# A four-layer graph network on one core: layer 2 with transposed scores and a constant shift, and direct row sums for the last graph

## The chip, the cores and the metric

The kernel runs on one core of a Trainium2 chip. A core has TensorE (matrix products, PE in the profile, with its weight loads as PEld), VectorE (DVE), ScalarE (ACT), GpSimd (POOL) and SyncE (SP, which only issues transfers here), and 16 DMA engines. The engines run their own queues in order and wait for one another by semaphores. The metric is the device time of one launch in microseconds: before the change 3004.08 us, the median of three runs (3002.78 to 3010.93).

## The reference

There are 32 graphs of 512 nodes with 256 features. All share one 512x512 adjacency matrix, about 6% full and with a full diagonal. Four attention layers follow one another, each wrapped as x = layernorm(x + layer(x)). Layer 0 is an 8-head transformer block with a masked softmax and a small MLP. Layers 1 and 3 score an edge by a sum of two node terms under a leaky ReLU (one head in layer 1, four in layer 3). Layer 2, which the change rewrites, multiplies the features:

```python
h1 = inp @ W1; h2 = inp @ W2; h3 = inp @ W3
e = einsum('bnd,bmd->bnm', h1, h2)
e = leaky_relu(e, 0.2)
e = where(adj > 0, e, -1e12)
attention = softmax(e, axis=-1)
return relu(attention @ h3)
```

A softmax does not change when one constant is subtracted from all scores of a row; which constant is used matters only for the range of the exponentials.

## The kernel before

**Staging.** The weights, the adjacency (as edge_t, the transposed 0/1 matrix in bf16, and mask, a large number where there is no edge) and a few constants are prepared once by `prepare`. Then the function `graph` describes one graph: load x, run `layer0` to `layer3`, each followed by `normalise`, store. A graph's 512 nodes lie in four chunks of 128 partitions (NC = 4), its 256 features in two (KC = 2). All intermediates stay on chip, in numbered buffers of a few kinds: "p" (8 buffers of 128x2048, for the attention weights), "t", "y", "v", "e", "rs" and others, and eight PSUM banks of 128x512.

**Order of the work.** Nothing is issued while a layer is described. Each call of `plan` appends an operation with an engine, an assumed duration in ns, what it reads and writes, and, for transfers, an assumed time to landing (`lag`). `Plan.place` then simulates the engines and buffers and picks at each step the operation that can start first, with ties and urgency decided by a due time: the graph's number times PACE plus the due time of this operation within a graph, which a lone placement of one graph stretched by the table TENTHS gives. Up to five graphs (WAYS) are open at a time. START delays the first graphs' first operations, LAST shifts the due times of the last graphs, STAY is a penalty for a change of TensorE's tiling mode (operations carry a `tiling` number). So each engine's instruction order is fixed when the kernel is built; on the chip an engine only waits for semaphores.

**Layer 2** (line 1166): xT is transposed by TensorE (line 866), qT is its product with the combined matrix l2m = -W1 W2^T (line 879), v its product with W3 (line 893). For each chunk c of query nodes, line 1180 makes the negated scores with queries on the partitions; ScalarE makes 0.2 times them (line 1183), VectorE takes the minimum (line 1186), then adds the mask and finds each row's minimum in one instruction (line 1188), which is the row's maximum of the true scores. ScalarE takes the exponential with that as its bias and adds up each row (line 1193), and VectorE inverts the sum (line 1196). The second product needs the keys on the partitions, so 16 TensorE transposes a graph (line 1203) and four ScalarE evacuations (line 854) turn p into pT; line 1214 multiplies pT by v, and line 1219 applies the ReLU and the inverted sum.

**Layer 1** already builds its weights with keys on the partitions and gets row sums from a column of ones beside v (lines 1141, 1155, 1160).

**Row sums in layers 0 and 3.** Their exponentials also have keys on the partitions. The partial tiles p of a head group are added by accumulating DMAs from GpSimd (`add_dma`, line 934), in two levels; then a product with a one-hot matrix `pick` sums over the partitions (lines 1042 and 1269), followed by an evacuation, transposes (line 947) and a reciprocal.

**Range check.** The kernel keeps running minima of 0/1 tests in `fit`, `far` and `odd`; at the end they become one flag (line 1325 on), and if it is set, the slower `general_path` computes everything again.

Of the kernel before, what the change touches and what calls it, by code (L numbers as in the profile page):

```python
# [9 lines left out]
FP = mybir.dt.float32  # L10
# [7 lines left out]
P = 128  # L18
# [4 lines left out]
R_MIN, R_MAX = 1e-30, 1e20  # L23
H0, H3 = 8, 4
# [3 lines left out]
PACE = 90.76  # L28
START = (0, 0, 60.35, 91.65, 156.14)
LAST = ()  # L30
STAY = 3.96
TENTHS = (0, 30.43, 93, 94.94, 170.51, 206.64, 280.32, 312.71, 390.11, 381.83, 480.02)
# [411 lines left out]
class Plan:  # L444
# [62 lines left out]
    def place(self, urgency, ways, stay=0.0, run=True):  # L507


        held_by = {g: self.profile(g) for g in {self.ops[0].graph, self.ops[-1].graph}}  # L510
# [12 lines left out]
        def safe(op, kind, new):  # L523
            spare = len(free[kind]) - len(new)
            if spare < 0:
                return False
            have = spare
            for g in order:
                mine = held.get((g, kind), [])
                have += len(mine)  # L530
                if g == op.graph:
                    have += len(new)
                    mine = mine + new
                r, rows = front[g], held_by.get(g, held_by[self.ops[-1].graph])[kind]
                ahead = sorted(s.first for s in mine if s.first > r)
                for i, stop in enumerate(ahead + [len(rows)]):
                    if stop > r and max(rows[r:stop]) + len(ahead) - i > have:
                        return False
                    r = max(r, stop)
                if g == op.graph:  # L540
                    return True
# [70 lines left out]
def fast_path(  # L612
# [63 lines left out]
    nc.gpsimd.memset(eps, EPS)  # L676
    ones = const.tile([P, P], FP, name="ones")
# [47 lines left out]
    odd = keep("odd", [P, NC])  # L725

    def prepare():
        def load(dst, to, src, lag=3000):
            def run():
                with nc.allow_non_contiguous_dma(reason="columns, once"):  # L730
                    nc.sync.dma_start(to(T(dst[0] if isinstance(dst, tuple) else dst)), src)
            plan(SP, 450, run, [], [dst], lag=lag)
# [29 lines left out]
        for m in range(NC):  # L762
            bank = Slot("bank")

            def run(bank=bank, m=m):
                for c in range(NC):
                    nc.tensor.transpose(T(bank)[:, c * P:(c + 1) * P],
                                        T(edges)[:, c, m * P:(m + 1) * P], ident)
            plan(PE, 440, run, [edges], [bank])
            dve(690, lambda bank=bank, m=m: nc.vector.tensor_copy(T(edge_t)[:, m, :], T(bank)),  # L770
                [bank], [(edge_t, m)])

# [20 lines left out]
        for c in range(NC):  # L793
            off = Slot("e")
            dve(690, lambda c=c: nc.vector.tensor_scalar(
                T(mask)[:, c, :], T(raws[c // 2])[:, c % 2, :].bitcast(I32), 0.0, BIG, ALU.is_le, ALU.mult),
                [(raws[c // 2], c)], [(mask, c)])
            dve(690, lambda c=c, off=off: nc.vector.tensor_tensor(
                T(off), T(edges)[:, c, :], T(raws[c // 2])[:, c % 2, :].bitcast(I32), ALU.not_equal),
                [edges, (raws[c // 2], c)], [off])  # L800
            dve(690, lambda c=c, off=off: nc.vector.tensor_reduce(
                T(odd)[:, c:c + 1], T(off), mybir.AxisListType.X, ALU.max), [off], [(odd, c)])
# [34 lines left out]
        for k in range(KC):  # L837
            bank = Slot("bank")

            def run(bank=bank, k=k):  # L840
# [6 lines left out]
                T(l2m)[:, k, :], T(bank)[:, :C], AF.Copy, scale=-1.0), [bank], [(l2m, k)])  # L847
        load(l2w3, lambda t: t, rows(l2_w3))
        scored(l3w, l3_w, l3_a, H3)
# [154 lines left out]
    def layer0(xs):  # L1004
# [7 lines left out]
        oT, sm, totals = Slot("t"), Slot("bank"), []  # L1012
        for g in range(KC):
            av, ps = Slot("bank"), []
            for m in range(NC):
# [14 lines left out]
                if m % 2:  # L1030
                    add_dma(ps[m - 1], p)
                if m == 3:
                    add_dma(ps[0], ps[2])
                total = ps[0]

            totals.append(total)
            evac(oT, lambda t, g=g: t[:, g, :], av, lambda b: b, N, [(oT, g)])

        def run():
            for g, p in enumerate(totals):  # L1040
                for j in range(J):
                    nc.tensor.matmul(T(sm)[j * 32:(j + 1) * 32, :], pick[:, g, :], T(p)[:, j, :],  # L1042
                                     start=(g == 0), stop=(g == KC - 1))
        plan(PE, 1740, run, totals, [sm], tiling=2)
# [3 lines left out]
        def check():  # L1048
            r = T(rinv)[:, :NC * H0]
            nc.vector.scalar_tensor_tensor(fit, r, R_MIN, fit, ALU.is_gt, ALU.min)  # L1050
            nc.vector.scalar_tensor_tensor(fit, r, R_MAX, fit, ALU.is_lt, ALU.min)
        dve(370, check, [rinv], [], True)
# [113 lines left out]
    def layer2(xs):  # L1166
        xT = transposed(xs)
        qT, v, p, pT, y = Slot("t"), Slot("v"), Slot("p"), Slot("p"), Slot("y")
        for k in range(KC):
            project_t(l2m, k * P, xT, qT, k)  # L1170
        project(xT, l2w3, 0, C, v)
        rinvs = []
        for c in range(NC):
            bank, lo, es = Slot("bank"), Slot("e"), Slot("e")
            low, tot, rinv = Slot("rs"), Slot("rs"), Slot("rs")
            rinvs.append(rinv)

            def run(bank=bank, c=c):
                for k in range(KC):
                    nc.tensor.matmul(T(bank), T(qT)[:, k, c * P:(c + 1) * P], T(xT)[:, k, :],  # L1180
                                     start=(k == 0), stop=(k == KC - 1))
# [3 lines left out]

            dve(690, lambda bank=bank, lo=lo, es=es: nc.vector.tensor_tensor(
                T(es), T(bank), T(lo), ALU.min), [bank, lo], [es])
            dve(780, lambda es=es, low=low, c=c: nc.vector.tensor_tensor_reduce(
                T(es), T(es), T(mask)[:, c, :], 1.0, TOP, ALU.add, ALU.min, T(low)[:, 0:1]),
                [es, (mask, c)], [es, low], True)  # L1190

            def exp(es=es, low=low, tot=tot, rinv=rinv, c=c):
                nc.scalar.activation(T(p)[:, c, :], T(es), AF.Exp, bias=T(low)[:, 0:1],
                                     scale=-1.0, accum_out=T(tot)[:, 0:1])
            act(935, exp, [es, low], [(p, c), tot])
            dve(160, lambda tot=tot, rinv=rinv: nc.vector.reciprocal(
                T(rinv)[:, 0:1], T(tot)[:, 0:1]), [tot], [rinv])
        for m in range(NC):
            bank = Slot("bank")

            def run(bank=bank, m=m):
                for c in range(NC):
                    nc.tensor.transpose(T(bank)[:, c * P:(c + 1) * P],  # L1203
                                        T(p)[:, c, m * P:(m + 1) * P], ident)
            plan(PE, 440, run, [p], [bank])
            evac(pT, lambda t, m=m: t[:, m, :], bank, lambda b: b, N, [(pT, m)])
        for c0 in range(0, NC, 2):
            bank = Slot("bank")

            def run(bank=bank, c0=c0):  # L1210
                for j in range(2):
                    c = c0 + j
                    for m in range(NC):
                        nc.tensor.matmul(T(bank)[:, j * C:(j + 1) * C],  # L1214
                                         T(pT)[:, m, c * P:(c + 1) * P], T(v)[:, m, :C],
                                         start=(m == 0), stop=(m == NC - 1))
            plan(PE, 3470, run, [pT, v], [bank])
            for j in range(2):
                act(470, lambda bank=bank, j=j, c=c0 + j: nc.scalar.activation(  # L1219
                    T(y)[:, c, :], T(bank)[:, j * C:(j + 1) * C], AF.Relu,  # L1220
                    scale=T(rinvs[c])[:, 0:1]), [bank, rinvs[c0 + j]], [(y, c0 + j)])
            add(y, y, xs, c0)
        return y

    def layer3(xs):
# [4 lines left out]
        e1, e02 = gates(q, H3, G)  # L1230
        for k in range(KC):
            av = Slot("bank")
            for m0 in range(0, NC, 2):
# [25 lines left out]
                if m0 == 0:  # L1259
                    total = p  # L1260
                else:
                    add_dma(total, p)
                    add_dma(total, None)

            totals.append(total)
            evac(oT, lambda t, k=k: t[:, k, :], av, lambda b: b, N, [(oT, k)])
        def run():
            for h in range(H3):
                nc.tensor.matmul(T(sm)[32 * h:32 * h + 32, :], pick[:, 0, :],  # L1269
                                 T(totals[h // 2])[:, h % 2, :], start=True, stop=True)  # L1270
        plan(PE, 870, run, totals, [sm], tiling=2)
# [15 lines left out]
    def graph(b):  # L1287
        xs = Slot("x")
# [3 lines left out]
        for layer in (layer0, layer1, layer2, layer3):  # L1292
            y = layer(xs)
            xs = Slot("x")
            normalise(y, xs)
# [81 lines left out]
```

## Time and profile before

One profiled execution spans 3009.1 us.

| engine | busy us | instructions |
|---|---|---|
| TensorE | 2903.1 | 14698 |
| VectorE | 2361.4 | 4138 |
| ScalarE | 1963.8 | 4359 |
| GpSimd | 951.3 | 875 |

Layer 2's own groups, from the page and the list of groups by line:

| line | engine, operation | count | busy us | mean ns |
|---|---|---|---|---|
| 1180 | TensorE scores | 512 | 238.7 | 599 |
| 1183 | ScalarE 0.2 x | 128 | 73.1 | 598 |
| 1186 | VectorE minimum | 128 | 87.2 | 681 |
| 1188 | VectorE mask and row minimum | 128 | 88.6 | 692 |
| 1193 | ScalarE exponential | 128 | 91.2 | 712 |
| 1203 | TensorE transposes | 512 | 73.8 | 280 |
| 854 | ScalarE evacuations into p | 128 | 72.2 | 598 |
| 1214 | TensorE output product | 1024 | 230.2 | 382 |

The row minimum and the exponential have a second record each, which reads an accumulator (81 and 190 ns). A 512-column fp32 product shows as two records, a transpose as one. Records of TensorE overlap, so a mean of a record is longer than the spacing of two; the chain of waits, which lists pieces of work one after another, gives the spacing.

### The profile page before, as it was taken

To read this page: it belongs to the slowest core of one execution; us is meant where nothing else is said; L and a number is where in the kernel's file an instruction comes from. 1 tells how busy PE (TensorE), PEld (TensorE's weight loads), DVE (VectorE), ACT (ScalarE), POOL (GpSimd) and SP (SyncE) were. 2 spreads that over 40 slices of the span, in tenths; PEclk is the share of its full clock that TensorE was granted. 3 is DMA by queue.
4 is the path that set the end of the run, shared out by engine and by line. 5 is a ranking of instruction groups with operands and counts; after the bars stand their busy time and mean duration, and the time that the engine had idled before them with its cause. 6 is when DMAs were issued, how large, how long until landed. Compare 5 with 4: busy or idle time off the path is not lost.

```text
span 3009.1 us, 40990 instructions
## 1 busy us (share of the span) xinstructions
PE 2903.1 (96%) x14698; PEld 1649.3 (55%) x14698; DVE 2361.4 (78%) x4138; ACT 1963.8 (65%) x4359; POOL 951.3 (32%) x875
## 2 busy tenths in 40 slices
PE   7989999999999999999999999999999999999983
PEld 3455555555555555555555555555555555555551
DVE  4467778888888888887888888888788888888773
ACT  3566766666766666776666776666776666676552
POOL 0222343323333322333322333332233332333211
PEclk9999999999999999999999999999999999999996
DMA  5644755666655566565566566566566566665434
GB/s 142 130 90 97 154 121 118 137 144 133 140 131 116 128 147 140 129 136 118 127 148 137 123 140 132 116 142 137 127 142 132 118 135 144 135 139 125 90 83 97
DMA packets 95155, 385.20 MB, mean 128 GB/s; under 512 B 8928, under 2 KB 44896, under 8 KB 58080
## 3 DMA queue, kind: packets, MB, share of 16 engines
q0 software_dynamic: 46080, 302.01, 51.2%
q1 hardware_dynamic: 48864, 80.49, 7.9%
q8 instruction: 118, 1.93, 0.3%
q14 instruction: 93, 0.76, 0.1%
HBM read 63.38 MB, written 17.10 MB: 27 GB/s over the span
## 4 chain that ended last, share of the span: by engine, by line
PE 91%; DMA 3%; DVE 3%; ACT 1%; issue 1%; POOL 0%; SPq 0%; DVEq 0%; ACTq 0%
PE bank L893 15%; PE bank L879 11%; PE bank L996 9%; PE bank L1025 8%; PE bank L1155 8%; PE bank L1214 7%; PE bank L1254 7%; PE bank L1180 7%; PE bank L866 5%; PE bank L1082 4%; PE bank L1070 4%; PE bank L1042 2%; PE bank L979 2%; PE bank L1203 2%; PE bank L947 1%; PE bank L1269 1%
## 5 line engine op out<-in xcount | busy, mean ns | idle before, releaser
L934 POOL DMA_DIRECT2D p<-p x320 | 289.3, 906 | 1304.0 <-issue 352.9
L1018 DVE TENSOR_TENSOR p<-p,edge_t 128x2048 f32<-128x2048 f32 x256 | 602.3, 2354 | 82.9 <-ACT p L1000 82.9
L1000 ACT ACTIVATE p<-bank 128x512 f32<-128x512 f32 x1024 | 560.1, 597 | 138.5 <-PE bank L996 138.3
L854 ACT ACTIVATE t<-bank 128x512 f32<-128x512 f32 x640 | 372.5, 594 | 364.9 <-PE bank L1254 146.7
L924 POOL TENSOR_TENSOR y<-y,x 128x512 f32<-128x512 f32 x192 | 339.0, 1771 | 358.7 <-ACT y L1219 174.1
L907 DVE BATCH_NORM_STATS2 st<-y 128x6 f32<-128x256 f32 x768 | 315.1, 410 | 66.6 <-POOL y L924 59.0
L996 PE MATMUL bank<-t,t 32*128 32x512 f32 x2048 | 296.3, 645 | 0.0
L1245 DVE TENSOR_TENSOR p<-p,edge_t 128x2048 f32<-128x2048 f32 x128 | 292.8, 2287 | 3.3
L917 ACT ACTIVATE x<-y,rs,rs 128x256 f32<-128x256 f32 x512 | 284.0, 596 | 8.4 <-DVE rs L914 8.1
L1238 DVE TENSOR_SCALAR p<-p,e,e 128x512 f32<-128x512 f32 x512 | 249.6, 540 | 43.3 <-DMA p<-row 37.3
L1025 PE MATMUL bank<-p,v 128*32 128x512 f32 x2048 | 270.1, 610 | 10.6 <-DVE p L1018 10.4
L1155 PE MATMUL bank<-v,p 128*128 128x257 f32 x1024 | 247.9, 387 | 9.3 <-DVE rs L914 7.0
L1254 PE MATMUL bank<-p,v 128*64 128x512 f32 x1024 | 238.5, 607 | 11.7 <-DVE p L1245 11.7
L854 ACT ACTIVATE v<-bank 128x512 f32<-128x512 f32 (+2 forms) x384 | 171.8, 455 | 112.8 <-PE bank L893 109.5
L1180 PE MATMUL bank<-t,t 128*128 128x512 f32 x512 | 238.7, 599 | 0.0
L879 PE MATMUL bank<-t,wqkv 128*128 128x512 f32 x512 | 232.4, 603 | 0.0
L1214 PE MATMUL bank<-v,p 128*128 128x256 f32 x1024 | 230.2, 382 | 0.0
L1155 PEld LDWEIGHTS bank<-v,p 128*128 128x128 f32 x1024 | 188.9, 192 | 70.6 <-issue 26.5
L1214 PEld LDWEIGHTS bank<-v,p 128*128 128x128 f32 x1024 | 191.9, 190 | 48.4 <-ACT t L854 20.5
L917 ACT ACTIVATE y<-y,rs,rs 128x256 f32<-128x256 f32 x256 | 138.9, 595 | 60.4 <-DVE rs L914 60.4
L996 PEld LDWEIGHTS bank<-t,t 32*128 32x128 f32 x2048 | 82.5, 184 | 167.4 <-issue 76.6
L866 PEld LDWEIGHTS bank<-ident,x 128*128 128x128 f32 x1024 | 117.8, 143 | 101.0 <-issue 59.3
(116 smaller groups left out, 4479.6 us busy)
## 6 DMA issues: line engine op xcount, KB each, us to landing
p<-p POOLq DMA_DIRECT2D x256, 1024.0 KB, 7.6
p<-row SPq DMA_DIRECT2D x32, 1024.0 KB, 9.4
p<-p POOLq DMA_DIRECT2D x64, 512.0 KB, 5.3
x<-in_x_dram SPq DMA_DIRECT2D x32, 512.0 KB, 4.0
out_dram<-x SPq DMA_DIRECT2D x32, 512.0 KB, 4.8
e<-row SPq DMA_DIRECT2D x32, 256.0 KB, 6.5
t<-in_adj_dram SPq DMA_DIRECT2D x4, 256.0 KB, 6.5
wqkv<-in_L_gnn_w_qkv_dram SPq DMA_DIRECT2D x1, 768.0 KB
```

Of the source, the lines that this page charges most:

```text
L854: act(170 + n * 0.84, lambda: nc.scalar.activation(to(T(dst)), frm(T(src)), AF.Copy), [src], writes)
L879: nc.tensor.matmul(T(bank), T(w)[:, i, col:col + P], T(xT)[:, i, :], start=(i == 0), stop=(i == KC - 1))
L893: nc.tensor.matmul(T(bank)[:, j * width:(j + 1) * width], T(xT)[:, k, (c0 + j) * P:(c0 + j + 1) * P], T(w)[:, k, col:col + width], start=( ...
L917: act(600, lambda c=c: nc.scalar.activation(T(dst)[:, c, :], T(y)[:, c, :], AF.Identity, bias=T(nm)[:, c:c + 1], scale=T(rs)[:, c:c + 1]), ...
L996: nc.tensor.matmul(T(banks[j]), T(kT)[r, g, m * P:(m + 1) * P], T(qT)[r, g, :], start=True, stop=True)
L1000: act(600, lambda j=j: nc.scalar.activation(T(p)[:, j, :], T(banks[j]), AF.Exp, scale=1.0 / math.sqrt(D0)), [banks[j]], [(p, j)])
L1018: dve(2420, lambda p=p, m=m: nc.vector.tensor_tensor(T(p), T(p), T(edge_t)[:, m, :].unsqueeze(1).to_broadcast([P, J, N]), ALU.mult), [p, ( ...
L1025: nc.tensor.matmul(T(av)[j * D0:(j + 1) * D0, :], T(v)[:, m, h * D0:(h + 1) * D0], T(p)[:, j, :], start=(m == 0), stop=(m == NC - 1))
L1155: nc.tensor.matmul(T(bank)[:, :C + 1], T(p)[:, m, c * P:(c + 1) * P], T(v)[:, m, 2:C + 3], start=(m == 0), stop=(m == NC - 1))
L1180: nc.tensor.matmul(T(bank), T(qT)[:, k, c * P:(c + 1) * P], T(xT)[:, k, :], start=(k == 0), stop=(k == KC - 1))
L1214: nc.tensor.matmul(T(bank)[:, j * C:(j + 1) * C], T(pT)[:, m, c * P:(c + 1) * P], T(v)[:, m, :C], start=(m == 0), stop=(m == NC - 1))
L1254: nc.tensor.matmul(T(av)[i * D3:(i + 1) * D3, :], T(q)[:, m0 + m, 2 * H3 + h * D3:2 * H3 + (h + 1) * D3], T(p)[:, 2 * m + i, :], start=(m0 ...
```

## The change

**Layer 2** is computed with keys on the partitions from the start: the score product swaps its two operands (and l2m loses its minus sign), so that p is already what the second product needs. The transposes and evacuations of p go, and so does one "p" buffer. A row's maximum would now lie across partitions; a constant, SHIFT = 72, is subtracted in every row instead. The row sum comes from a column of ones in v, as in layer 1. Since a constant may overflow or underflow where a row's own maximum cannot, the reciprocals of the sums are tested against limits, and so is the size of W3's columns.

**The last graph** sums the rows of layers 0 and 3 directly on TensorE, all partial tiles by `pick`, without the accumulating DMAs (`at_once`; `skip` keeps the operations' ranks the same as in other graphs).

**The order**: the planner's constants are new, the assumed landing time of the weights is 15 us instead of 3 (where a load names no other), and the mask is made from edge_t.

```diff
-PACE = 90.76
-START = (0, 0, 60.35, 91.65, 156.14)
-LAST = ()
-STAY = 3.96
-TENTHS = (0, 30.43, 93, 94.94, 170.51, 206.64, 280.32, 312.71, 390.11, 381.83, 480.02)
+PACE = 88.54
+START = (0, 19.02, 60.35, 66.56, 231.93)
+LAST = (-45.23,)
+STAY = 3.33
+TENTHS = (0, 19.01, 80, 84.85, 160.81, 189.49, 259.9, 297.79, 374.53, 362.85, 470.13)
...
-        def load(dst, to, src, lag=3000):
+        def load(dst, to, src, lag=15000):
...
+            dve(400, lambda m=m: nc.vector.tensor_scalar(
+                T(mask)[:, m, :], T(edge_t)[:, m, :], 1.0, BIG, ALU.subtract, ALU.mult),
+                [(edge_t, m)], [(mask, m)])
...
+            for k in range(KC):
+                nc.tensor.matmul(T(bank)[:, :C], ones, T(sq)[:, k * C:(k + 1) * C],
+                                 start=(k == 0), stop=(k == KC - 1))
+        plan(PE, 870, run, [sq], [bank])
...
+        def sums(g, p, start, stop):
+            for j in range(J):
+                nc.tensor.matmul(T(sm)[j * 32:(j + 1) * 32, :], pick[:, g, :], T(p)[:, j, :],
+                                 start=start, stop=stop)
+
+        def collect(g, m, ps):
+
+            if at_once:
+                for c in (m - 1, m):
+                    plan(PE, 870, lambda c=c: sums(g, ps[c], g == 0 and c == 0,
+                                                   g == KC - 1 and c == NC - 1),
+                         [ps[c]], [sm], tiling=2)
+                skip(m - 1)
+            else:
+                add_dma(ps[m - 1], ps[m])
+                if m == 3:
+                    add_dma(ps[0], ps[2])
...
     def layer2(xs):
...
+        plan(POOL, 110, lambda: nc.gpsimd.memset(T(v)[:, :, C:C + 1], 1.0), [xT], [(v, "one")])
         project(xT, l2w3, 0, C, v)
...
-                    nc.tensor.matmul(T(bank), T(qT)[:, k, c * P:(c + 1) * P], T(xT)[:, k, :],
+                    nc.tensor.matmul(T(bank), T(xT)[:, k, m * P:(m + 1) * P], T(qT)[:, k, :],
...
-                T(es), T(bank), T(lo), ALU.min), [bank, lo], [es])
-            dve(780, lambda es=es, low=low, c=c: nc.vector.tensor_tensor_reduce(
-                T(es), T(es), T(mask)[:, c, :], 1.0, TOP, ALU.add, ALU.min, T(low)[:, 0:1]),
-                [es, (mask, c)], [es, low], True)
-
-            def exp(es=es, low=low, tot=tot, rinv=rinv, c=c):
-                nc.scalar.activation(T(p)[:, c, :], T(es), AF.Exp, bias=T(low)[:, 0:1],
-                                     scale=-1.0, accum_out=T(tot)[:, 0:1])
-            act(935, exp, [es, low], [(p, c), tot])
-            dve(160, lambda tot=tot, rinv=rinv: nc.vector.reciprocal(
-                T(rinv)[:, 0:1], T(tot)[:, 0:1]), [tot], [rinv])
-        for m in range(NC):
+                T(es), T(bank), T(lo), ALU.max), [bank, lo], [es])
+            dve(690, lambda es=es, m=m: nc.vector.tensor_tensor(
+                T(es), T(es), T(mask)[:, m, :], ALU.add), [es, (mask, m)], [es], True)
+            act(600, lambda es=es, m=m: nc.scalar.activation(
+                T(p)[:, m, :], T(es), AF.Exp, bias=shift), [es], [(p, m)])
+        for c in range(NC):
...
-                for c in range(NC):
-                    nc.tensor.transpose(T(bank)[:, c * P:(c + 1) * P],
-                                        T(p)[:, c, m * P:(m + 1) * P], ident)
-            plan(PE, 440, run, [p], [bank])
-            evac(pT, lambda t, m=m: t[:, m, :], bank, lambda b: b, N, [(pT, m)])
...
+                for m in range(NC):
+                    nc.tensor.matmul(T(bank)[:, :C + 1], T(p)[:, m, c * P:(c + 1) * P],
+                                     T(v)[:, m, :C + 1], start=(m == 0), stop=(m == NC - 1))
+            plan(PE, 1740, run, [p, v], [bank])
+            dve(160, lambda bank=bank, c=c: nc.vector.reciprocal(
+                T(rinv)[:, c:c + 1], T(bank)[:, C:C + 1]), [bank], [(rinv, c)])
+            act(470, lambda bank=bank, c=c: nc.scalar.activation(
+                T(y)[:, c, :], T(bank)[:, :C], AF.Relu, scale=T(rinv)[:, c:c + 1]),
+                [bank, (rinv, c)], [(y, c)])
+            if c % 2:
+                add(y, y, xs, c - 1)
+        dve(250, lambda: within(T(rinv), R2_MIN, R2_MAX), [(rinv, c) for c in range(NC)], [], True)
...
-    def layer3(xs):
+    def layer3(xs, at_once):
...
-                if m0 == 0:
+                if at_once:
+                    plan(PE, 1740, lambda p=p, k=k, m0=m0: [sums(
+                        2 * k + i, p, 2 * m + i, m0 + m == 0, m0 + m == NC - 1)
+                        for m in range(2) for i in range(2)], [p], [sm], tiling=2)
+                    skip(2 if m0 else 0)
+                elif m0 == 0:
...
     def graph(b):
+
+        at_once = b == B - 1
```

More of the change, by code (lines that the diff above doesn't have):

```diff
@@ L23 @@
 R_MIN, R_MAX = 1e-30, 1e20
+SHIFT = 72.0
+R2_MIN, R2_MAX = 1.25e-37, 1e31
+V_MAX = 41.0
 H0, H3 = 8, 4
 WAYS = 5
-PACE = 90.76
-START = (0, 0, 60.35, 91.65, 156.14)
-LAST = ()
-STAY = 3.96
-TENTHS = (0, 30.43, 93, 94.94, 170.51, 206.64, 280.32, 312.71, 390.11, 381.83, 480.02)
+PACE = 88.54
[3 more added lines that the diff above has]
+TENTHS = (0, 19.01, 80, 84.85, 160.81, 189.49, 259.9, 297.79, 374.53, 362.85, 470.13)
 @with_exitstack
@@ L507, in place @@
     def place(self, urgency, ways, stay=0.0, run=True):
-        held_by = {g: self.profile(g) for g in {self.ops[0].graph, self.ops[-1].graph}}
+        held_by = {g: self.profile(g) for g in {op.graph for op in self.ops}}
         engines = {e: 0.0 for e in (PE, DVE, ACT, POOL, SP, DMA)}
@@ L533, in safe @@
                     mine = mine + new
-                r, rows = front[g], held_by.get(g, held_by[self.ops[-1].graph])[kind]
+                r, rows = front[g], held_by[g][kind]
                 ahead = sorted(s.first for s in mine if s.first > r)
@@ L676, in fast_path @@
     nc.gpsimd.memset(eps, EPS)
+    shift = const.tile([P, 1], FP, name="shift")
+    nc.gpsimd.memset(shift, -SHIFT)
     ones = const.tile([P, P], FP, name="ones")
@@ L724, in fast_path @@
     edge_t, mask = keep("edge_t", [P, NC, N], BF), keep("mask", [P, NC, N], BF)
-    odd = keep("odd", [P, NC])
+    odd = keep("odd", [P, NC + 1])
     def prepare():
-        def load(dst, to, src, lag=3000):
+        def load(dst, to, src, lag=15000):
             def run():
@@ L794, in prepare @@
             off = Slot("e")
-            dve(690, lambda c=c: nc.vector.tensor_scalar(
-                T(mask)[:, c, :], T(raws[c // 2])[:, c % 2, :].bitcast(I32), 0.0, BIG, ALU.is_le, ALU.mult),
-                [(raws[c // 2], c)], [(mask, c)])
             dve(690, lambda c=c, off=off: nc.vector.tensor_tensor(
@@ L846, in prepare, with run @@
             act(400, lambda bank=bank, k=k: nc.scalar.activation(
-                T(l2m)[:, k, :], T(bank)[:, :C], AF.Copy, scale=-1.0), [bank], [(l2m, k)])
+                T(l2m)[:, k, :], T(bank)[:, :C], AF.Copy), [bank], [(l2m, k)])
         load(l2w3, lambda t: t, rows(l2_w3))
+        sq, bank, wide = Slot("e"), Slot("bank"), Slot("e")
+        act(600, lambda: nc.scalar.activation(T(sq), flat(T(l2w3)), AF.Square), [l2w3], [sq])
+        def run():
+            for k in range(KC):
+                nc.tensor.matmul(T(bank)[:, :C], ones, T(sq)[:, k * C:(k + 1) * C],
+                                 start=(k == 0), stop=(k == KC - 1))
+        plan(PE, 870, run, [sq], [bank])
+        dve(400, lambda: nc.vector.tensor_scalar(
+            T(wide)[:, :C], T(bank)[:, :C], V_MAX ** 2 / C, None, ALU.is_gt), [bank], [wide])
+        dve(400, lambda: nc.vector.tensor_reduce(
+            T(odd)[:, NC:NC + 1], T(wide)[:, :C], mybir.AxisListType.X, ALU.max),
+            [wide], [(odd, NC)])
         scored(l3w, l3_w, l3_a, H3)
@@ L1002, in exps, with within, skip, layer0 @@
                 [banks[j]], [(p, j)])
-    def layer0(xs):
+    def within(r, low, high):
+        seen = fit[:, :r.shape[-1]]
+        nc.vector.scalar_tensor_tensor(seen, r, low, seen, ALU.is_gt, ALU.min)
+        nc.vector.scalar_tensor_tensor(seen, r, high, seen, ALU.is_lt, ALU.min)
+    def skip(n):
+        for _ in range(n):
+            plan(DMA, 0, None)
+    def layer0(xs, at_once):
         xT = transposed(xs)
@@ L1030, in layer0 @@
                 if m % 2:
[L1031 to L1036, printed above, removed]
-            evac(oT, lambda t, g=g: t[:, g, :], av, lambda b: b, N, [(oT, g)])
[L1039 to L1044, printed above, removed]
+                    collect(g, m, ps)
+            evac(oT, lambda t, g=g: t[:, g, :], av, lambda b: b, N, [(oT, g)])
+            totals.append(ps[0])
+        if at_once:
+            skip(1)
+        else:
+            plan(PE, 1740, lambda: [sums(g, p, g == 0, g == KC - 1) for g, p in enumerate(totals)],
+                 totals, [sm], tiling=2)
         rinv = rinv0(sm)
         t = heads_out(oT, rinv, H0)
[L1048 to L1052, printed above, removed]
+        dve(370, lambda: within(T(rinv)[:, :NC * H0], R_MIN, R_MAX), [rinv], [], True)
         for c0 in range(0, NC, 2):
@@ L1167, in layer2, with run @@
         xT = transposed(xs)
-        qT, v, p, pT, y = Slot("t"), Slot("v"), Slot("p"), Slot("p"), Slot("y")
+        qT, v, p, y, rinv = Slot("t"), Slot("v"), Slot("p"), Slot("y"), Slot("rs")
         for k in range(KC):
             project_t(l2m, k * P, xT, qT, k)
+        plan(POOL, 110, lambda: nc.gpsimd.memset(T(v)[:, :, C:C + 1], 1.0), [xT], [(v, "one")])
         project(xT, l2w3, 0, C, v)
-        rinvs = []
-        for c in range(NC):
+        for m in range(NC):
             bank, lo, es = Slot("bank"), Slot("e"), Slot("e")
-            low, tot, rinv = Slot("rs"), Slot("rs"), Slot("rs")
-            rinvs.append(rinv)
-            def run(bank=bank, c=c):
+            def run(bank=bank, m=m):
                 for k in range(KC):
-                    nc.tensor.matmul(T(bank), T(qT)[:, k, c * P:(c + 1) * P], T(xT)[:, k, :],
+                    nc.tensor.matmul(T(bank), T(xT)[:, k, m * P:(m + 1) * P], T(qT)[:, k, :],
                                      start=(k == 0), stop=(k == KC - 1))
@@ L1195, in layer2 @@
-            act(935, exp, [es, low], [(p, c), tot])
-            dve(160, lambda tot=tot, rinv=rinv: nc.vector.reciprocal(
-                T(rinv)[:, 0:1], T(tot)[:, 0:1]), [tot], [rinv])
-        for m in range(NC):
-            bank = Slot("bank")
-            def run(bank=bank, m=m):
-                for c in range(NC):
-                    nc.tensor.transpose(T(bank)[:, c * P:(c + 1) * P],
-                                        T(p)[:, c, m * P:(m + 1) * P], ident)
-            plan(PE, 440, run, [p], [bank])
-            evac(pT, lambda t, m=m: t[:, m, :], bank, lambda b: b, N, [(pT, m)])
@@ L1207, in layer2 @@
[L1207 to L1222, printed above, removed]
+                T(es), T(bank), T(lo), ALU.max), [bank, lo], [es])
@@ new lines, in layer2, with run @@
+            dve(690, lambda es=es, m=m: nc.vector.tensor_tensor(
[3 more added lines that the diff above has]
+        for c in range(NC):
+            bank = Slot("bank")
+            def run(bank=bank, c=c):
+                for m in range(NC):
+                    nc.tensor.matmul(T(bank)[:, :C + 1], T(p)[:, m, c * P:(c + 1) * P],
[8 more added lines that the diff above has]
+                add(y, y, xs, c - 1)
@@ L1230, in layer3, with sums @@
         e1, e02 = gates(q, H3, G)
+        def sums(h, p, part, start, stop):
+            nc.tensor.matmul(T(sm)[32 * h:32 * h + 32, :], pick[:, 0, :], T(p)[:, part, :],
+                             start=start, stop=stop)
         for k in range(KC):
@@ L1258, in layer3 @@
                 plan(PE, 1770, run, [q, p], [av], tiling=3)
-                if m0 == 0:
+                if at_once:
+                    plan(PE, 1740, lambda p=p, k=k, m0=m0: [sums(
[3 more added lines that the diff above has]
+                elif m0 == 0:
                     total = p
@@ L1263, in layer3 @@
                     add_dma(total, None)
-            totals.append(total)
+                    totals.append(total)
             evac(oT, lambda t, k=k: t[:, k, :], av, lambda b: b, N, [(oT, k)])
[L1267 to L1271, printed above, removed]
+        if at_once:
+            skip(1)
+        else:
+            plan(PE, 870, lambda: [sums(h, totals[h // 2], h % 2, True, True) for h in range(H3)],
+                 totals, [sm], tiling=2)
         t = heads_out(oT, rinv3(sm), H3)
@@ L1292, in graph @@
         for layer in (layer0, layer1, layer2, layer3):
-            y = layer(xs)
+            y = layer(xs, at_once) if layer in (layer0, layer3) else layer(xs)
             xs = Slot("x")
```

## The prediction

> **What bounds the kernel now.** I read the page's engine shares first, then the slices, the chain that ended last, the chain in one steady stretch, the table of stretches and last the waits at both ends.
>
> ```profile
> span 3009.1 us, 40990 instructions
> PE 2903.1 (96%) x14698; PEld 1649.3 (55%) x14698; DVE 2361.4 (78%) x4138; ACT 1963.8 (65%) x4359; POOL 951.3 (32%) x875
> ...
> PE   7989999999999999999999999999999999999983
> ...
> PE 91%; DMA 3%; DVE 3%; ACT 1%; issue 1%; POOL 0%; SPq 0%; DVEq 0%; ACTq 0%
> ```
>
> TensorE is busy for 2903 of 3009 us and carries 91% of the chain; only the first slices and the last two have gaps. VectorE is next at 78%.
>
> ```profile
> 0.00:300.00 300.00, 263.57 (x1288) 140.83 (x1288) 177.80 (x318) 167.27 (x357) 63.63 (x72) 0.95 0.52 115
> 300.00:2800.00 2500.00, 2493.34 (x12796) 1419.61 (x12800) 2054.94 (x3556) 1709.97 (x3805) 842.31 (x756) 1.00 0.62 133
> 2800.00:3009.00 209.00, 146.21 (x618) 88.84 (x610) 128.68 (x266) 86.53 (x199) 45.36 (x47) 0.84 0.38 88
> ```
>
> This is the table of busy time by stretch: after the length come PE, PEld, DVE, ACT, POOL, then the granted clock. The middle has 6.7 us of idle TensorE in 2500; the start has 36 us and the end 63 us. So the middle is bound by TensorE's work and nothing else, and the two ends by latency. In the middle the output store of line 1296 starts at 2594.36 and 2683.64 us: one graph takes 89.28 us, and VectorE fills 82% of it (2054.94 / 2500), ScalarE 68%.
>
> The steady part of the chain prices TensorE's pieces by their spacing:
>
> ```profile
> 1457.55 1.85 PE bank L1042 x16
> 1459.41 1.02 PE bank L1203 x8
> 1460.43 0.44 PE bank L947 x4
> 1460.87 0.44 PE bank L1203 x4
> ...
> 1463.91 0.44 PE bank L1203 x4
> ...
> 1470.71 7.11 PE bank L1214 x32
> ...
> 1480.96 1.93 PE bank L1155 x8
> ...
> 1483.32 1.74 PE bank L1155 x8
> ```
>
> Each row is start, length, line and records. Four transposes of line 1203 take 0.44 us; the first eight, right after a tiled piece, take 1.02 = 0.88 + 0.14.
>
> [...] 0.14 us above, and the same step at line 1155 (1.93 against 1.74, so 0.14 to 0.19). [...] here the stretches from 2920 us on were granted 0.56 to 0.83, and eight records of line 1254 took 3.46 us at 2954 us against 1.87 in the middle. [...] a transpose record indeed shows 273 ns where the spacing is 110, so I price TensorE by spacing.
>
> **Part 1, layer 2, in all 32 graphs.** Removed from TensorE: 16 transposes (line 1203), 4 x 0.44 = 1.76 us a graph, 56.3 us in all. Two checks: the page's chain gives line 1203 2% of 3009 us (60 us), and PE's records in 300 to 2700 us are 416, 26 graphs of 16. The score matmuls only swap operands: the same 8 of 128x512. The output matmuls stay 16 but grow from 256 to 257 columns. Line 1155 already runs 257: 1.74 x 4 = 6.96 us; line 1214 takes 7.11 less 0.14 for the switch, 6.97. I take the growth as zero.
>
> VectorE: four 692 + 81 ns min-reduces (line 1188) become four plain adds of the bf16 mask. No row has this very shape; from below, a quarter of the 2354 ns product with edge_t (line 1018), 588 ns, from above 692 (line 1096). I take 690. That saves 0.33 us a graph; the two added range checks (192 and 222 ns by lines 1050 and 1051) give 0.41 back, and the reciprocal costs 155 to 159 either way. VectorE stays at about 75 us a graph, under the 87.5 us that TensorE will need. ScalarE: four evacuations of 598 ns go, and the exponential falls from 712 + 190 to about 597 ns: 2.39 + 1.22 = 3.6 us less. GpSimd gets a memset of 475 ns at 32% load. All these lie beside TensorE's work and are costed at nothing.
>
> Wait added: the Relu of line 1219 and its reciprocal now wait for the ones-column in the same bank. The reciprocal sits in VectorE's queue behind masked products of up to 2.35 us and the Relu waits for it; behind the Relu, GpSimd's residual add. Line 1160 has the same pattern in layer 1 (79.6 us of VectorE idle before it over 32 graphs), with TensorE saturated anyway. Cost: zero in the middle, up to 2.4 us in the last graph.
>
> **Part 2, the last graph's row sums.** Before, they go through accumulating DMAs, and the chain shows that wait at the end:
>
> ```profile
> 2962.28 3.70 PE bank L1254 x8
> ...
> 2969.33 9.07 DMA p<-p
> ...
> 2978.68 6.48 DMA p<-p
> ...
> 2985.30 2.06 PE bank L1269 x8
> ...
> 2995.63 0.35 DVE st L907
> ```
>
> TensorE's last attention records end at 2970.1 us (timeline), the sums at 2987.4: 17.3 us. Now the sums follow the attention directly: four matmuls onto two column groups, priced like line 1254, 1.73 us at full clock and 3.5 at half. The path shortens by 13.8 to 15.5 us; I take 14.5. Layer 0 of that graph pays instead: eight sum groups of 0.86 us (line 1025 or 1269 without the switch) in place of 1.72, +5.2 us of saturated TensorE. Layer 3's other three groups (5.2 us) fall between 2904 and 2966 us, where TensorE idles. Net: -9.3 us.
>
> **Part 3, the order of work.** Between 2900 and 2970 us TensorE idles about 20 us, as one graph's chain (attention, residual, normalise, gates, row broadcast at 2944.8) runs alone; graph 30's last store is issued at 2975.9, graph 31's at 3000.7. LAST pulls graph 31 forward by 45 us of due time, so that it overlaps with graph 30. Bounds: nothing to 25 us (20 idle plus the lost clock); I take 10. From the final sums to the last instruction (22 us) nothing can fill TensorE.
>
> At the start TensorE stands 9.0 us (waits at line 831) for the weights of layer 2, placed as if they landed in 3 us. With 15 us the planner puts them behind graph 0's projections, which then stood queued until 25.8 us. Bounds: 0 to 12 us, since later stalls (7.0 us at line 1155, 9.9 at line 1025) may take part of it back; I take 6. The added checks of W3 are two 256-column matmuls (0.22 us a record) and a few short passes, beside the loads; the mask now comes from edge_t with as many passes.
>
> The retuned order can also change the number of tiling switches. I count about 30 a graph in the chain from 1400 to 1489 us; three more or fewer, at 0.14 us, over 32 graphs is 13 us either way. I take zero.
>
> **Sum.** 56.3 + 9.3 + 10 + 6 = 81.6; 3004.1 - 81.6 = 2922 us.
>
> **Rivals.** A, the forecast: 2922 us, chance 0.55. B: the ends do not shrink and the order is looser (three more switches): 3004 - 56 - 9 + 13 = 2952, chance 0.2. For it: the ends are latency, and static orders are planned on modelled times. Against: the waits at both ends are named, and one is removed outright. C: fewer switches and ends at their bounds: 3004 - 56 - 9 - 13 - 25 - 12 = 2889, chance 0.19. Against: all must come right together. D: the freed 1.76 us turns into a VectorE wait, because a queued product of 2.35 us stands before the max or the reciprocal in each graph: +0.6 us x 32 = 19, at the other ends nothing, 3023 us, slower; chance 0.04. For it: VectorE's share rises to 84 to 85%. Against: line 1160 shows such waits hidden. E: a row sum leaves the checked range, so the general path follows: all work twice, over 5900 us; chance 0.02. I evaluated the reference's layer-2 scores: they reach 155.7, and the reciprocals of the shifted row sums run from 4.4e-37 to 9.5e28, inside 1.25e-37 and 1e31, by a factor of 3.5 on the narrow side; W3's largest squared column mean is 2.27 / 256 against a limit of 6.57.
>
> **How the numbers follow.** The time is A's. The range runs from C's end at 2889 to just above B, 2956, which leaves out D, E and the outer tails of B and C. Faster by over 0.3% (below 2995) is A, B and C: 0.94. Within 0.3%: 0.02, part of D. Slower: 0.04, the rest.
>
> **What would show it.** Stores of line 1296 some 87.5 us apart in the middle (89.28 now), TensorE still over 99% busy there; no transposes in layer 2; PE busy near 2858 us (2903 - 56 + 11). At the end no DMA in the chain after the last attention records, and 22 to 25 us from there to the end. At the start no 9 us wait at line 831. A pace of 88.5 or more would tell of more switches or new waits; TensorE under 98% busy in the middle would refute the whole argument.

## The result, and the profile after

The changed kernel takes 3060.04 us (median of four runs, 3057.57 to 3062.98), the kernel before, run again beside it, 3005.73. The ratio is 1.018 (95% interval 1.016 to 1.020): slower by 54 us, where the forecast was 2922 us.

The page of the changed kernel shows the same TensorE time as before although 512 transposes are gone:

```profile
span 3060.2 us, 39724 instructions
PE 2904.2 (95%) x14262; PEld 1625.2 (53%) x14262; DVE 2302.4 (75%) x4076; ACT 1890.2 (62%) x4104; POOL 914.5 (30%) x898
...
PE   7999999999999999999999999999999999999995
...
L886 PE MATMUL bank<-ident,x 128*128 128x128 f32 x1024 | 166.4, 301 | 96.2 <-DMA x<-in_x_dram 88.5
```

The last row is new among the costly groups: line 886, the transposes of x (line 866 before), had 96 us of idle time ahead of it, 88.5 of them until a load of x from memory landed. The page's chain is of no use this time; it breaks off after the last few instructions on ScalarE and VectorE.

The table of busy time by stretch (columns as in the prediction) shows where:

```profile
0.00:300.00 300.00, 269.29 (x1340) 142.31 (x1341) 191.53 (x337) 170.52 (x358) 72.43 (x84) 0.96 0.55 122
300.00:2800.00 2500.00, 2417.92 (x11927) 1357.64 (x11926) 1927.27 (x3366) 1589.60 (x3454) 781.27 (x752) 0.98 0.61 129
```

The start lost less than before (31 us idle instead of 36). The middle, which had 6.7 us of idle TensorE, has 82, and a granted clock of 0.98 instead of 1.00. The table of waits for TensorE in the middle names one cause:

```profile
PE bank L886 <- DMA x<-in_x_dram: 80.4, 24, 4.6
```

That is 24 waits of up to 4.6 us, 3.35 on average, in 24 of the 27 graphs of the middle. One of the longer ones in the timeline, first TensorE, then the table of two short stretches:

```profile
1461.70 1.90 PE L1236 MATMUL bank<-v,p 128*128 128x257 f32 x8
1467.58 1.97 PE L886 MATMUL bank<-ident,x 128*128 128x128 f32 x8 [3.99 <-DMA x<-in_x_dram]
1469.34 3.44 PE L1236 MATMUL bank<-v,p 128*128 128x257 f32 x8
```

```profile
1463.60:1467.50 3.90, 0.00 (x0) 0.00 (x0) 3.87 (x6) 0.00 (x0) 0.00 (x0) 0.76 0.38 131
1467.50:1472.60 5.10, 5.02 (x16) 4.36 (x17) 4.19 (x7) 1.20 (x2) 0.33 (x1) 0.51 0.18 51
```

TensorE stands for 3.9 us, and then works for 5.1 us at a granted clock of 0.51: eight records of line 1236 take 3.44 us there and 1.90 ahead of it. So a late load is paid twice, here by 4 us of waiting and about 2.5 us of half speed. The trace's record of the clock has one stretch at 0.5 for each of the 24 waits, 17 of 3.4 us and seven of 6.8 us; while TensorE works in them it loses 47.4 us in all, 2.0 us a wait.

Why is the load late? The timelines of the transfer queues (SP issues loads and stores, POOL the accumulating adds, that is the DMAs of `add_dma`), after the change:

```profile
1450.23 0.39 SPq L1330 DMA_DIRECT2D out_dram<-x  x1
1457.94 0.38 SPq L1323 DMA_DIRECT2D x<-in_x_dram  x1
```

```profile
1449.40 0.86 POOL L954 DMA_DIRECT2D p<-p  x1 [11.49 <-DVE p L1266]
1456.90 0.85 POOL L954 DMA_DIRECT2D p<-p  x1 [6.53 <-DMA p<-p]
```

and in the kernel before:

```profile
1430.77 0.39 SPq L1296 DMA_DIRECT2D out_dram<-x  x1
1436.38 0.38 SPq L1289 DMA_DIRECT2D x<-in_x_dram  x1
```

```profile
1423.92 0.86 POOL L934 DMA_DIRECT2D p<-p  x1 [4.95 <-DVE st L907]
1438.35 0.92 POOL L934 DMA_DIRECT2D p<-p  x1 [13.57 <-PE bank L866]
```

A finished graph's store frees the x buffer that the load fills, so the load waits for the store. Before the change, the adds lay further from both: 6.8 us ahead of the store and 2.0 us behind the load. After it, an add of 1 MB is issued 0.8 us ahead of the store, and the next one, which waits for the first to land, 1.0 us ahead of the load. From store to load it takes 7.7 us in this graph instead of 5.6 (medians over the graphs 7.7 and 6.0). The list of DMA issues, whose last column is the median from issue to landing, has the loads before and after:

```profile
x<-in_x_dram SPq DMA_DIRECT2D x32, 512.0 KB, 4.0
x<-in_x_dram SPq DMA_DIRECT2D x32, 512.0 KB, 8.3
```

TensorE's first use of this x in the kernel before:

```profile
1445.74 1.03 PE L866 MATMUL bank<-ident,x 128*128 128x128 f32 x8
```

There it had some 5 us to spare (1436.38 + 4.0 = 1440.4). Now x comes 17.4 us after the store's issue, and TensorE is there after 13.4 (1463.60 - 1450.23); before, it came after 15.0 (1445.74 - 1430.77). The planner had counted 3 us for the store to land and 9 for the load (`lag` in `graph`), some 13 us with both issues: enough for a load that runs into an add, not for a store that does so too.

It takes both. Of the 27 graphs of the middle, two had the add only 0.1 to 0.2 us ahead of the store, and there the load followed the store after 3.0 us; one had the add 9 us ahead of the load, which then landed in 4.1 us. These three took 87.6 to 87.7 us from store to store and had no wait; the other 24 took 92.3 to 95.6 us.

The accounts close. Stores are (2846.83 - 347.08) / 27 = 92.58 us apart in the middle; 80.4 / 27 = 2.98 us of that is the wait and 47.4 / 27 = 1.76 us the lost clock. Without both, 87.84 us would be left, against 87.5 forecast.

### The profile page after: what moved, and what is told of

Same layout as the page of the kernel before. It is cut to its first block, busy times and chain, and to the rows that moved or that the text cites. A ratio compares the mean times of both kernels' runs of the same rounds, so it can differ in the third digit from the quotient of the medians.

```text
span 3060.2 us, 39724 instructions
## 1 busy us (share of the span) xinstructions
PE 2904.2 (95%) x14262; PEld 1625.2 (53%) x14262; DVE 2302.4 (75%) x4076; ACT 1890.2 (62%) x4104; POOL 914.5 (30%) x898
## 5 line engine op out<-in xcount | busy, mean ns | idle before, releaser
L954 POOL DMA_DIRECT2D p<-p x310 | 270.7, 900 | 1441.4 <-DVE p L1266 287.5
L1068 DVE TENSOR_TENSOR p<-p,edge_t 128x2048 f32<-128x2048 f32 x256 | 586.4, 2292 | 126.4 <-ACT p L1020 126.3
L1020 ACT ACTIVATE p<-bank 128x512 f32<-128x512 f32 x1024 | 547.9, 597 | 88.1 <-PE bank L1016 87.9
L944 POOL TENSOR_TENSOR y<-y,x 128x512 f32<-128x512 f32 x192 | 322.9, 1684 | 455.3 <-ACT y L1241 230.3
L1273 DVE TENSOR_TENSOR p<-p,edge_t 128x2048 f32<-128x2048 f32 x128 | 293.4, 2293 | 4.2
L1197 PE MATMUL bank<-v,p 128*128 128x257 f32 x1024 | 256.0, 395 | 16.4 <-DVE p L1190 9.1
L1236 PE MATMUL bank<-v,p 128*128 128x257 f32 x1024 | 270.0, 417 | 0.0
L886 PE MATMUL bank<-ident,x 128*128 128x128 f32 x1024 | 166.4, 301 | 96.2 <-DMA x<-in_x_dram 88.5
L1197 PEld LDWEIGHTS bank<-v,p 128*128 128x128 f32 x1024 | 189.1, 194 | 104.4 <-issue 41.6
L874 ACT ACTIVATE v<-bank 128x264 f32<-128x264 f32 (+2 forms) x384 | 173.1, 461 | 106.1 <-PE bank L913 101.7
L1236 PEld LDWEIGHTS bank<-v,p 128*128 128x128 f32 x1024 | 209.0, 212 | 53.3 <-ACT t L874 20.5
L886 PEld LDWEIGHTS bank<-ident,x 128*128 128x128 f32 x1024 | 131.0, 154 | 159.6 <-DMA x<-in_x_dram 90.1
```

What stands on the lines that cost most here:

```text
L874: act(170 + n * 0.84, lambda: nc.scalar.activation(to(T(dst)), frm(T(src)), AF.Copy), [src], writes)
L886: nc.tensor.transpose(T(bank)[:, (2 * k + c) * P:(2 * k + c + 1) * P], T(src)[:, c0 + c, k * P:(k + 1) * P], ident)
L944: pool(1500 if row is None else 1850, lambda: nc.gpsimd.tensor_tensor(T(dst)[:, w, :], T(a)[:, w, :], T(b)[:, w, :] if row is None else T( ...
L1020: act(600, lambda j=j: nc.scalar.activation(T(p)[:, j, :], T(banks[j]), AF.Exp, scale=1.0 / math.sqrt(D0)), [banks[j]], [(p, j)])
L1068: dve(2420, lambda p=p, m=m: nc.vector.tensor_tensor(T(p), T(p), T(edge_t)[:, m, :].unsqueeze(1).to_broadcast([P, J, N]), ALU.mult), [p, ( ...
L1197: nc.tensor.matmul(T(bank)[:, :C + 1], T(p)[:, m, c * P:(c + 1) * P], T(v)[:, m, 2:C + 3], start=(m == 0), stop=(m == NC - 1))
```

## The experiments

**One more x buffer.** The load goes to a buffer that has been free for a long time; every engine keeps its order of instructions.

```diff
+    spare = [const.tile([P, NC, C], FP, name="x_5")]
...
+        def load_x(xs=xs):
+            tiles = buffers["x"]
+            tiles[xs.index], spare[0] = spare[0], tiles[xs.index]
+            nc.sync.dma_start(T(xs), x[b].rearrange("(c p) d -> p c d", p=P))
+        plan(SP, 450, load_x, [], [(xs, c) for c in range(NC)], lag=9000)
```

> The changed kernel with one more x buffer: the order of instructions on every engine stays, but a graph's load goes to a buffer that has been free for a long time, so that it no longer waits for the store ahead of it to land (7.7 us from the store's issue to the load's). Theory X (late x loads: some 3.0 us of idle TensorE a graph and some 2 us lost to the half clock after it): the waits before line 886 vanish, the granted clock in the middle goes from 0.98 back to 1.00, the stores come about 87.5 us apart, and the time is 3060 - 27 x 5.0 = about 2925 us (2915 to 2940). Rival Y (the transposed layer 2 or the order of work is slower in itself, and the x wait only sits where TensorE would wait anyway): the wait moves to another line and the time stays above 3040. Rival Z (only the wait counts, the half clock is there for another reason): 3060 - 80 = 2980.

Measured: 2932.84 us, ratio to the kernel before 0.974 (0.9725 to 0.9758). The load is now issued 0.5 us behind the store (1404.60 and 1405.11 us). It still lands late, in 9.6 us, but TensorE does not need it by then. The middle of the table by stretch:

```profile
300.00:2700.00 2400.00, 2398.36 (x12147) 1338.77 (x12146) 1944.25 (x3404) 1609.78 (x3503) 796.29 (x764) 1.00 0.63 135
```

Idle TensorE is down to 1.6 us in 2400, the clock is 1.00, and stores are (2633.02 - 1404.60) / 14 = 87.74 us apart. Theory X holds; Y and Z fall. This version beats both kernels. It also shows that a load which lands late does no harm by itself, if it doesn't have to wait for the store.

**Work instead of waiting.** Four products of constants ahead of the first transposes of x, from the fifth graph on.

```diff
+                for _ in range(filler if c0 == 0 else 0):
+                    nc.tensor.matmul(T(bank), ident, flat(T(wqkv))[:, :N], start=True, stop=True)
                 for k in range(KC):
```

> The changed kernel with four 512-column products of constants put into TensorE's queue ahead of the first transposes of x in each graph from the fifth on, 3.4 us at full clock, into the bank that the transposes then overwrite. The x load is as late as before; TensorE works where it stood idle. Theory X with the half clock as a part of the loss: the clock in the middle returns to about 1.00, the idle time before line 886 falls from 80 us to under 20, and the time falls although 28 x 3.4 = 96 us of work are added: 3060 + 96 - 80 - 50 = about 3026 us (3010 to 3040). If the half clock costs nothing (rival Z): 3060 + 16 = 3076.

Measured: 3032.45 us, ratio 1.007 (1.0055 to 1.0089), 28 us less than the changed kernel with 96 us more of work. The load is as late as ever (issue to landing 8.0 us). The wait shrinks and the clock returns:

```profile
PE bank L889 <- DMA x<-in_x_dram: 3.7, 5, 1.0
```

```profile
300.00:2700.00 2400.00, 2395.23 (x11848) 1330.15 (x11848) 1876.79 (x3290) 1547.58 (x3370) 779.68 (x740) 1.00 0.62 130
```

The half clock is thus a cost of its own and goes with the long idle stretches: with only waits of up to 1.0 us left, the granted clock of the middle reads 1.00, against 0.98 with the waits of 2.9 to 4.6 us.

**Smaller adds.** The accumulating DMAs move a quarter of the bytes (half in the second level); their number and all orders stay.

```diff
-            a, b = (T(dst), T(src)) if src else (T(dst)[:, 0:2, :], T(dst)[:, 2:4, :])
+            a, b = (T(dst)[:, 0:1, :], T(src)[:, 0:1, :]) if src else (T(dst)[:, 0:1, :], T(dst)[:, 2:3, :])
```

> The changed kernel with the accumulating DMAs of the row sums cut to a quarter of their bytes (half for the second level); three quarters of the row sums are left out. The number of transfers and the order of all instructions stay. Theory C (the store and the load of x are late because each queues behind a 1 MB accumulating transfer that was issued just ahead of it): from the store's issue to the load's issue 7.7 us falls to about 4, the load's landing from 8.3 to about 4, the waits before line 886 vanish, and the time is about 2925 us (2910 to 2945). If the store and the load are slow for another reason: 7.7 and 8.3 us stay, and so do the waits and 3060 us.

Measured: 2935.68 us, ratio 0.975 (0.9733 to 0.9766). From the store's issue to the load's is now 4.1 us (1407.27 to 1411.38), and the page's list of DMA issues, with its last column from issue to landing, has the loads of x at 4.2 us:

```profile
p<-p POOLq DMA_DIRECT2D x310, 256.0 KB, 3.3
...
x<-in_x_dram SPq DMA_DIRECT2D x32, 512.0 KB, 4.2
```

No wait for x is left in the middle. The run also moves less in all, but the amount alone does not make loads late: the kernel before kept the DMA engines as busy in the middle as the changed one (0.62 and 0.61), and its loads landed in 4.0 us. So it is the collision with the adds that makes the loads late, and taking away either the collision or the dependence on the store brings the same time within 3 us. How the transfers hinder one another inside the DMA engines is not shown.

**The transposes put back**, with nothing waiting for them, in the kernel with the spare buffer.

```diff
+                for m in range(NC):
+                    nc.tensor.transpose(T(bank)[:, m * P:(m + 1) * P],
+                                        T(p)[:, c, m * P:(m + 1) * P], ident)
```

> The kernel with one more x buffer, and in layer 2 four transposes of p put back ahead of each output product, into the bank that the product then overwrites: 16 a graph, as the kernel before had them, but with nothing waiting for them. Where TensorE is the bound again, they cost their full 16 x 0.11 = 1.76 us a graph, 56 us in all over the kernel with one more x buffer: about 2981 us if that one is at 2925. If TensorE's work is not what sets the time there, less than 20 us.

Measured: 2986.23 us, ratio 0.992 (0.9901 to 0.9934): 53.4 us over the spare buffer alone, 1.67 us a graph.

**The parts at the two ends**, each undone in the kernel with the spare buffer.

```diff
-        at_once = b == B - 1
+        at_once = False
```

> The kernel with one more x buffer, with the last graph's row sums through the accumulating DMAs as in all other graphs; the order is the same up to the last graph. By the prediction's part 2 the direct sums are worth 14.5 - 5.2 = 9.3 us at the end: the ratio to the kernel before rises from 0.974 to about 0.977 (2942 us where the other is at 2933). If the other idle stretches at the end take the saving back, it stays within 0.001 of 0.974.

Measured: 2942.45 us, ratio 0.977 (0.9755 to 0.9788), 9.6 us slower. The timeline at the end shows the old wait again:

```profile
2918.70 2.05 PE L1258 MATMUL bank<-p,pick 128*32 128x512 f32 x8 [11.85 <-DMA p<-p]
```

```diff
-        def load(dst, to, src, lag=15000):
+        def load(dst, to, src, lag=3000):
```

> The kernel with one more x buffer, with the weights' assumed landing time back at 3 us instead of 15. By the prediction's part 3 the 9 us wait at the start comes back and 0 to 12 us are lost, 6 as the middle: ratio to the kernel before about 0.976. If the start is bound by the latency of the first graphs whatever the order, less than 2 us (0.974 to 0.975).

Measured: 2943.56 us, ratio 0.977 (0.9756 to 0.9789), 10.7 us slower. The wait at the start is back in the table of waits:

```profile
PE bank L837 <- DMA y<-in_L_gnn_W_dram: 11.3, 1, 11.3
```

```diff
-LAST = (-45.23,)
+LAST = ()
```

> The kernel with one more x buffer, with LAST empty, so that the last graph is not pulled forward; the order is the same up to the last three graphs. By the prediction's part 3 this costs 0 to 25 us, 10 as the middle: ratio to the kernel before about 0.977. If it costs nothing, 0.974.

Measured: 2949.28 us, ratio 0.979 (0.9777 to 0.981), 16.4 us slower. The intervals of the first two of these ratios touch or overlap that of the spare buffer alone, since the kernel before varies by 11 us; the third lies clear of it. The four times of each run lie within some 4 us, and 7.9 us or more above the highest of the spare buffer alone. These runs and that one were measured at different times, with the kernel before at 3011.61 and 3011.41 us, so the sizes are good to a few us.

**The spare buffer in the kernel before,** by the same edit.

> The kernel before with the same one more x buffer, its order unchanged. Its x loads are issued 5.6 us after the store and land in 4.0, and TensorE waits only 3.9 us for them in the middle: the time falls by 0 to 6 us, ratio 0.998 to 1.000. If the kernel before also lost time to late x loads in a way that its profile hides, the ratio falls below 0.995.

Measured: 3006.51 us against 3011.61, ratio 0.998 (0.9973 to 0.999). The buffer is worth 5 us there and 127 in the changed kernel (132 by the two ratios, 1.018 and 0.974, since the changed kernel was measured beside a somewhat faster run of the kernel before): the late loads are no general weakness but belong to the new order.

**The order's constants exchanged** (PACE, START, LAST, STAY and TENTHS), one run of each.

> The changed kernel with the order's constants (PACE, START, LAST, STAY, TENTHS) of the kernel before. If the new layer 2 brings its saving in any reasonable order: 3060 us or less, near 2950 if the x loads then come in time. If the constants belong to one set of operations and durations, since the order is a greedy choice by due times: far above both kernels, over 3150 us, with TensorE idle in the middle for many reasons.

> The kernel before with the order's constants of the changed one. If these constants are better in themselves: under 3004 us. If they only fit the new layer 2: slower than before, some 3050 to 3150 us.

Measured: 3324.12 us for the new code with the old constants, 3165.17 for the old code with the new ones, against 3012.21. With the old constants the wait for x is not among TensorE's long ones in the middle; others are:

```profile
PE bank L1257 <- DMA p<-p: 100.7, 25, 11.0
PE bank L1075 <- DVE p L1068: 60.6, 37, 3.7
```

The kernel before with the new constants does wait for x:

```profile
PE bank L866 <- DMA x<-in_x_dram: 38.8, 9, 5.6
```

So the new constants bring late loads without the new layer 2 as well. The order is a greedy choice by due times, and in these two runs the constants suit only the operations they were set for. So "layer 2 alone" cannot be read off such a run; experiments that keep the order and change one dependence can.

## Why the prediction was wrong

**The step that failed** is the first conclusion, "the middle is bound by TensorE's work and nothing else", carried over to the new order. It was true of the trace of before, and the kernel with the spare buffer shows that the forecast pace was right (87.74 against 87.5 us). But the new order was priced by its tiling switches alone, at 0.14 us each, an estimate from eight transposes that took 1.02 us right after a tiled piece against 0.88 elsewhere: "I take zero". That term measured 127 us, the difference between the changed kernel and the same order with a spare buffer: 80 us of waits for x and 47 us of lost clock. The switches nearly stayed put, 31 a graph in the timeline against 30. Two of the prediction's own signs of being wrong came up: a pace of 92.58 us, above 88.5, and TensorE busy for 96.7% of the middle, under 98%. It had seen a granted clock of 0.56 to 0.83, but only at the end of the kernel, from 2920 us on.

**The rivals named the wrong engine.** D let the freed time turn into a wait on VectorE, at 19 us; TensorE's waits for VectorE in the middle are 1.0 us in all (line 1075). No rival looked at transfers. The profile of before had the signs. The load of x waits for a store in 27 graphs, 153.9 us in all (5.7 us each, where the code assumes 3), and one add of 1 MB takes 7.6 us to land:

```profile
SPq L1289 <- DMA out_dram<-x: 153.9, 27, 6.9
p<-p POOLq DMA_DIRECT2D x256, 1024.0 KB, 7.6
```

The spare time ahead of TensorE's use of x, some 5 us, is shorter than that. Whoever moves the order can move such a transfer by several us.

**What the runs confirm.** Part 1: the transposes are worth 53.4 us, forecast 56.3, and the wider product costs nothing (mean of line 1237 in the kernel with the spare buffer 383 ns, 382 before). VectorE's mask add measured 692 ns for the 690 taken; its 75 us a graph were put somewhat high (the table of before gives 2054.94 / 2500 x 89.28 = 73.4 us) and measured 71.1. ScalarE's exponential was mis-sized: 713 ns for the expected 597, since only the accumulator's record went; it is hidden. TensorE's busy time with the spare buffer is 2855.2 us, forecast 2858. Part 2: 9.6 us, forecast 9.3. Part 3: 16.4 us for the order at the end and 10.7 for the start, forecast 10 and 6, both inside their bounds. The whole with the spare buffer is 2933 us, so the forecast's range held for a kernel whose inputs arrive in time.

The four parts, each undone alone, add up to 90 us, while the kernel with the spare buffer is 79 us faster than the kernel before. An estimate from the one more switch a graph, 32 x 0.14 us, covers some 4 us of the difference; for the rest, it stays open whether the parts overlap or the new order loses a little elsewhere.

## What to carry to other kernels

A trace says what bounds the kernel in that order of work; a change that re-plans the order keeps the prices of operations but none of the slacks. For each transfer on which the bound engine depends, read issue, landing and first use, and compare the slack with the longest transfer it could collide with; where the slack is smaller, put that case among the rivals and price it as (wait + lost clock) x number of graphs. A load that needs only a buffer should not wait for the store of the graph just finished: one buffer more made it safe here. A longer assumed landing time for the store in the planner is another way, which no run tried.

## What the runs showed of the hardware

An idle stretch of 3.9 us of TensorE was followed by 5.1 us at a granted clock of 0.51. In the changed kernel each of the 24 waits for x, 2.9 to 4.6 us of idle time, came with such a stretch, and the 80 us of waits cost about 127 us; in the kernel before, two idle stretches of 1.7 and 2.2 us in the middle came with none (granted clock 1.00). Work of no use in the same place (96 us of it) made the kernel 28 us faster.

The loads of x, most of them issued about 1 us behind an accumulating transfer of 1 MB from another engine's queue, took 8.3 us to land (the median), against 4.2 with the adds at a quarter. Where the store was issued 0.8 us behind such a transfer, the load that waits for it followed after 7.7 us (the median), 4.7 us later than the 3.0 of the two graphs where the store lay only 0.1 to 0.2 us behind it.
